# Byte adjacency for layers 1 and 3 of a four-layer graph network, and its float32r copy written in layer 1

## Chip, cores and metric

The kernel runs on one core of one Trainium2 chip. The metric is the device time of one execution in microseconds (us), the median of several. All runs quoted here were in the fast state: none took over 1.5% more than the fastest of the same kernel. A run of the kernel before accompanies every comparison on the same chip, because that kernel's median differs by up to 12 us between groups of runs (4558.7 to 4570.7 us; by 3.5 us between two groups on one chip).

## The reference

Four layers work on X (4096 x 256) and one adjacency matrix of zeros and ones (4096 x 4096), each followed by a residual addition and a normalisation. Cut to what matters here:

```python
def _L1_gnn_ref(x, adj, weight, bias):
    support = x @ weight
    A = DIAG_LAMBDA * jnp.diagonal(adj) + adj
    return A @ support + bias
# layer 2 uses the adjacency too: R = (adj + I) / rowsum, R @ X in two steps
def _L3_gnn_ref(x, adj, W, b):
    deg = jnp.sum(adj, axis=1, keepdims=True)
    agg = adj @ x / jnp.maximum(deg, 1.0)
    return jax.nn.relu(jnp.concatenate([x, agg], axis=-1) @ W + b)
# each layer: x = _layernorm(x + layer(x, ...))
```

Layer 0 is an attention over the edges with eight heads. Layer 2 does two steps of diffusion beside a top-p attention.

## The kernel before

The adjacency arrives as float32, in tiles transposed on the host. Layer 0's first pass (called pz below, after its product) loads it once and makes two things of it in device memory: a float32r copy `adjs` (67 MB), and bytes `nad` (16.8 MB) whose value, read as fp8, is 2^-5 for an edge. Layer 0's main part (acc) reads the bytes. Layers 1, 2 and 3 read `adjs`.

```python
# layer 0, first pass (in a loop over blocks b, pieces g)
a = work.tile([P, 2, G, P], F32, name="a", bufs=2)
for q in range(2):
    nc.sync.dma_start(a[:, q], self.adjt[b + q, :, g * G:(g + 1) * G, :])
ar = work.tile([P, 2, G, P], F32R, name="ar")              # two buffers
nc.vector.tensor_copy(ar, a)
nb = work.tile([P, G, 2, P], U8, name="nb")
for q in range(2):
    nc.scalar.mul(nb[:, :, q, :], a[:, q], float(FIFTH))
    nc.gpsimd.dma_start(self.adjs[b + q, :, g * G:(g + 1) * G, :], ar[:, q].bitcast(F32))
nc.gpsimd.dma_start(nad[it, :, g * G:(g + 1) * G, i:i + 2 * P], nb.rearrange("p g q i -> p g (q i)"))
# ... 32 products from ar into pz
# [cut: layer 0's main part, layer 2]

# adj_product, used by layers 1 and 2
for g in range(self.NB // G):
    a = pool.tile([P, G, P], F32R, name="adj_piece", bufs=bufs)
    nc.sync.dma_start(a.bitcast(F32), self.adjs[...])      # [cut: indices]
    for k in range(G):
        nc.tensor.matmul(ps, a[:, k, :], rhs(g * G + k)..., ...)

# layer 1, after the support product; row = the diagonal's row + bias
for b in range(NB):
    ps = psum.tile([P, 512], F32, name="ps_adj")
    self.adj_product(work, ps, b, lambda jc: XD[:, jc])
    xb = X[:, b:b + 1, :]
    nc.gpsimd.tensor_add(xb[:, 0], xb[:, 0], row)          # "row add"
    nc.vector.tensor_add(xb[:, 0], xb[:, 0], ps[:, :D])
    nc.vector.tensor_add(xb[:, 0], xb[:, 0], ps[:, D:])
    self.layernorm(work, xb, xb)

# layer 3, products of a block, and its closing
for g in range(NB // G):
    a = work.tile([P, G, P], F32R, name="adj_piece", bufs=8)
    nc.sync.dma_start(a.bitcast(F32), self.adjs[b, :, g * G:(g + 1) * G, :])
    for jc in range(g * G, min((g + 1) * G, NB - 1)):
        product(ps, a, jc)
def close(b, ps, a):
    product(ps, a, NB - 1)
    x = work.tile([P, 2, D], F32, name="x", bufs=3)
    nc.scalar.dma_start(x, self.xo[b])
    # [cut: scale on ScalarE, four VectorE operations, layernorm]
    nc.scalar.dma_start(out[:, b, :], y[:, 0])
```

Instructions are put in order by a scheduler, not taken in source order: a row add needs only X and `row`, so the scheduler may put all 32 of them ahead.

## Time and profile before

The kernel takes 4560.47 us (median of three, 4558.66 to 4562.25). The profiled run has a span of 4560.9 us and these stages, read from the first and last start of each product:

| stage | us |
|---|---|
| layer 0, first pass (pz, 4096 products) | 76.4 to 629.2: 552.8 |
| layer 0, main part (acc) | 647.8 to 1377.1: 729.3 |
| layer 1, first support product to last product | 1398.3 to 1691.9: 293.6 |
| layer 2, from there to its last product | 1691.9 to 4281.3: 2589.4 |
| layer 2's last product to layer 3's first | 6.9 |
| layer 3, first to last product | 4288.2 to 4548.9: 260.7 |
| after layer 3's last product | 12.0 |

The prediction below shows the slices, the windows and the waits. One more view is needed for layer 1, the timeline of the kernel before (start, length, engine, source line, operation, tiles, shapes, count, and in brackets the idle time before it and what ended it), first GpSimd's row adds, then the first VectorE instruction after its long idle time:

```profile
1447.23 22.11 POOL L660 TENSOR_TENSOR X<-X,row 128x256 f32<-128x256 f32 x32 [54.98 <-DVE row L654]
...
1469.38 0.29 DVE L769 COPY v<-ident 64x64 f32<-64x64 f32 x2 [15.39 <-POOL X L660]
```

All 32 row adds run in one burst of 22 us, and VectorE stands still for 15 us behind them, in front of a copy that already belongs to layer 2. The early layer 2 load of which the prediction speaks waits for the same burst.

### The profile page before, as it was taken

What the parts mean: (1) busy time and instruction counts of PE and PEld (TensorE: products, weight loads), DVE (VectorE), ACT (ScalarE), POOL (GpSimd) and SP (SyncE); (2) the same over time, 40 slices, a digit from 0 to 9 for tenths busy, and PEclk for the clock granted to TensorE, in tenths of its full rate; (3) what the DMA queues carried; (4) which work ended last, traced back from release to release, by engine and by line L of the source; (5) the groups of instructions that cost most, each with busy time, mean ns of one, the idle gap of its engine ahead of it and who ended that gap; (6) DMA issues with size and microseconds to landing.
All of it is one profiled execution on the core that took longest, in us unless ns stands there. A gap on an engine that the chain in (4) does not pass through costs nothing. (4 is left out here: it accounts for less than half of the span.)

```text
span 4560.9 us, 70953 instructions
## 1 busy us (share of the span) xinstructions
PE 4263.9 (93%) x25625; PEld 3423.7 (75%) x25625; DVE 3254.6 (71%) x7529; ACT 2630.8 (58%) x5373; POOL 458.0 (10%) x794
## 2 busy tenths in 40 slices
PE   8799989999997999999999999887999999999898
PEld 7799989999995876677777777664666666666676
DVE  6532349999993236977777777388989998999133
ACT  5433359998881015766666666267667767775100
POOL 1344420001102100000000000001010000000000
PEclk9999999999998999999999999998999999999899
DMA  5898982342212974012222222530121222222697
GB/s 162 289 312 305 309 303 77 113 147 67 63 62 77 317 261 150 26 62 92 85 80 79 78 81 94 194 111 27 60 73 65 76 74 79 78 79 77 223 318 253
DMA packets 312087, 624.21 MB, mean 137 GB/s; under 512 B 42406, under 2 KB 117926, under 8 KB 311718
## 3 DMA queue, kind: packets, MB, share of 16 engines
q1 hardware_dynamic: 197700, 423.31, 28.3%
q0 software_dynamic: 33344, 107.11, 6.6%
q10 hardware_dynamic: 80674, 89.06, 5.8%
q8 instruction: 207, 3.39, 0.3%
q14 instruction: 162, 1.33, 0.1%
HBM read 464.29 MB, written 155.06 MB: 136 GB/s over the span
## 5 line engine op out<-in xcount | busy, mean ns | idle before, releaser
L1180 PE MATMUL ps_a<-X,aT 128*128 128x256 f32 x4096 | 964.2, 387 | 28.9 <-ACT aT L1177 28.8
L1180 PEld LDWEIGHTS ps_a<-X,aT 128*128 128x128 f32 x4096 | 763.3, 191 | 294.7 <-ACT aT L1177 137.9
L242 PE MATMUL acc<-gm,gt 128*128 128x198 bf16 x8192 | 710.2, 250 | 37.7 <-issue 18.3
L242 PEld LDWEIGHTS <-gt 128*128 128x128 fp8e4 x8192 | 705.2, 98 | 42.7 <-issue 18.5
L234 ACT ACTIVATE sg<-lpb,nlc 128x1024 fp8e4<-128x1024 f32 x640 | 670.5, 1135 | 76.5 <-DVE gt L236 38.3
L450 PE MATMUL pz<-src,ar 128*128 128x264 f32 x4096 | 520.9, 290 | 32.5 <-DVE ar L439 26.0
L450 PEld LDWEIGHTS pz<-src,ar 128*128 128x128 f32 x4096 | 514.7, 192 | 38.6 <-DVE ar L439 31.3
L155 PE MATMUL ps_r<-XD,adj_piece 128*128 128x512 f32 x2048 | 509.9, 401 | 14.1 <-DMA adj_piece<-adjs 13.9
L1177 ACT COPY aT<-ps_tp 128x512 f32<-128x512 f32 x512 | 277.5, 583 | 360.3 <-PE ps_tp L1175 358.1
L915 ACT ACTIVATE ja<-e,nc 128x2048 uint8<-128x2048 f32 x240 | 478.7, 1995 | 0.5 <-issue 0.2
L155 PEld LDWEIGHTS ps_r<-XD,adj_piece 128*128 128x128 f32 x2048 | 382.7, 189 | 114.0 <-DMA adj_piece<-adjs 27.9
L842 PE MATMUL ps_logit<-kT,q 64*128 64x512 f32 x1024 | 462.5, 637 | 4.0 <-ACT e L846 3.9
L861 DVE SCALAR_TENSOR_TENSOR v<-e,c 128x4096 bf16<-128x4096 f32 x100 | 447.2, 4472 | 7.3 <-ACT c L889 6.5
L997 DVE MAX8 cand<-v 128x8 f32<-128x256 f32 x1024 | 360.6, 411 | 2.2
L83 POOL TENSOR_SCALAR ln_var<-ln_mv 128x1 f32<-128x1 f32 (+1 forms) x144 | 53.1, 369 | 3027.3 <-DVE ln_mv L81 2786.3
L1044 DVE SCALAR_TENSOR_TENSOR e<-e,edge 128x512 f32<-128x512 f32 x512 | 347.3, 746 | 1.5
L442 ACT ACTIVATE nb<-a 128x512 uint8<-128x512 f32 x256 | 159.2, 630 | 308.4 <-DMA a<-in_adjt_dram 270.7
L1175 PE MATMUL ps_tp<-ident,e 128*128 128x128 f32 x2048 | 273.3, 275 | 38.9 <-DVE e L1044 26.1
L993 DVE SCALAR_TENSOR_TENSOR v<-e,hi 128x2048 f32<-128x2048 f32 x128 | 300.9, 2351 | 1.7
L1175 PEld LDWEIGHTS ps_tp<-ident,e 128*128 128x128 f32 x2048 | 242.1, 142 | 77.3 <-DVE e L1044 29.5
L846 ACT ACTIVATE e<-ps_logit 128x1024 f32<-128x1024 f32 x256 | 261.2, 1021 | 49.4 <-PE ps_logit L842 34.6
L227 DVE TENSOR_SCALAR sg<-lpb,nlc 128x1024 fp8e4<-128x1024 f32 x384 | 273.6, 749 | 1.7
(300 smaller groups left out, 5079.0 us busy)
## 6 DMA issues: line engine op xcount, KB each, us to landing
adj_piece<-adjs SPq DMA_DIRECT2D x256, 512.0 KB
adj_piece<-adjs SPq DMA_DIRECT2D x512, 256.0 KB
a<-in_adjt_dram SPq DMA_DIRECT2D x256, 256.0 KB
adjs<-ar POOLq DMA_DIRECT2D x256, 256.0 KB, 5.1
na<-nad SPq DMA_DIRECT2D x64, 512.0 KB
nad<-nb POOLq DMA_DIRECT2D x128, 128.0 KB, 4.5
lpb<-lpd POOLq DMA_DIRECT2D x32, 512.0 KB, 4.0
xfd<-part ACTq DMA_DIRECT2D x63, 256.0 KB
```

Of the source, the lines that this page charges most:

```text
L155: nc.tensor.matmul(ps, a[:, k, :], rhs(jc).rearrange("p s d -> p (s d)"), start=(jc == 0 and own is None), stop=(jc == self.NB - 1))
L234: nc.scalar.activation(sg[:, k, :], lpb, AF.Sign, scale=-1.0, bias=nlc[:, jc, h:h + 1], saturate=False)
L242: nc.tensor.matmul(acc[:, q, :6 * C1], gt[:, k, q * P:(q + 1) * P], gm[:, jc, hh, :], start=(jc == 0 and q % 2 == 0), stop=(jc == NB - 1 a ...
L450: nc.tensor.matmul(pz[q][:, t, :W], ar[:, q, k, :], src[:, jc, t, s], start=(jc == 0 and s == 0), stop=(jc == NB - 1 and s == 1))
L842: nc.tensor.matmul(pl[:, s, :], q[s * A:(s + 1) * A, :], kT[s * A:(s + 1) * A, c * 512:(c + 1) * 512], start=True, stop=True)
L861: nc.vector.scalar_tensor_tensor(junk, e, c, e, op0=ALU.is_ge, op1=ALU.mult, accum_out=S)
L915: nc.scalar.activation(ja, e[:, s * HALF:(s + 1) * HALF], f, bias=nc1, accum_out=fs[:, i + s:i + s + 1])
L993: nc.vector.scalar_tensor_tensor(v, ec, hi, ec, op0=ALU.is_lt, op1=ALU.mult, accum_out=sb[:, s:s + 1])
L997: nc.vector.max(cand[:, 8 * j:8 * j + 8], v[:, k * 256:(k + 1) * 256])
L1044: nc.vector.scalar_tensor_tensor(ec, ec, edge[:, j:j + 1], ec, op0=ALU.is_ge, op1=ALU.mult)
L1175: nc.tensor.transpose(pt[:, k * P:(k + 1) * P], e[:, jc * P:(jc + 1) * P], self.ident)
L1180: nc.tensor.matmul(pa[:, :D], aT[:, k * P:(k + 1) * P], X[:, jc, :], start=(jc == 0), stop=(jc == NB - 1))
```

## The change

The intent is to move less data. Layer 0 no longer stores the float copy. Layer 1 loads the bytes (1 MB pieces, on the ScalarE queue), casts them on VectorE and ScalarE in turn, stores each cast piece as part of the float copy for layer 2 (128 stores of 512 KB on the SyncE queue), and multiplies from it. Layer 3 loads bytes and casts them as well; from its third block on, a block's last product also moves from the closing to the place before it. The core of the diff, with the lists that the two helpers fill and return cut:

```diff
 def adj_space(self):
+    self.nad = pool.tile([N // self.IT, P, NB, self.IT], U8, name="nad")
     self.adjs = pool.tile([self.NB, P, self.NB, P], F32, name="adjs")
+def bytes_of(self, pool, b, G=8):
+    for g in range(self.NB // G):
+        na = pool.tile([P, G, self.IT], U8, name="na", bufs=2 * (self.NB // G))
+        self.nc.scalar.dma_start(na, self.nad[b * P // self.IT, :, g * G:(g + 1) * G, :])
+def adj_pieces(self, pool, nas, b, G=8):
+    at = b * P % self.IT
+    if at == 0:
+        nas[:] = self.bytes_of(pool, b)
+    for g in range(self.NB // G):
+        a = pool.tile([P, G, P], F32R, name="adj_piece", bufs=2 * (self.NB // G))
+        edges = nas[g][:, :, at:at + P].bitcast(FP8)
+        if g % 2:
+            nc.scalar.mul(a, edges, 2.0 ** 5)
+        else:
+            nc.vector.tensor_scalar_mul(a, edges, 2.0 ** 5)
 # layer 0
-    nc.gpsimd.dma_start(self.adjs[b + q, :, g * G:(g + 1) * G, :], ar[:, q].bitcast(F32))
 # layer 1
+ahead = self.adj_pieces(work, nas, 0)
 for b in range(NB):
-    self.adj_product(work, ps, b, lambda jc: XD[:, jc])
+    now, ahead = ahead, None
+    for g, a in enumerate(now):
+        nc.sync.dma_start(self.adjs[b, :, g * 8:(g + 1) * 8, :], a.bitcast(F32))
+        ... # eight products from a
+    if b + 1 < NB:
+        ahead = self.adj_pieces(work, nas, b + 1)
 # layer 3
-    nc.sync.dma_start(a.bitcast(F32), self.adjs[b, :, g * G:(g + 1) * G, :])
+pieces = {b: self.adj_pieces(work, nas, b) for b in range(2)}
+    # in the loop: pieces[b + 2] = self.adj_pieces(work, nas, b + 2), ahead of close(b)
```

More of the change, by code (lines that the diff above doesn't have):

```diff
@@ L138, in adj_space @@
     def adj_space(self):
+        N, NB = self.N, self.NB
         pool = self.ctx.enter_context(self.tc.tile_pool(name="adjs", bufs=1, space=DRAM))
+        self.IT = min(1024, N)
+        self.nad = pool.tile([N // self.IT, P, NB, self.IT], U8, name="nad")
         self.adjs = pool.tile([self.NB, P, self.NB, P], F32, name="adjs")
@@ L156, in adj_product @@
                                  start=(jc == 0 and own is None), stop=(jc == self.NB - 1))
+    def bytes_of(self, pool, b, G=8):
+        nas = []
+        for g in range(self.NB // G):
+            na = pool.tile([P, G, self.IT], U8, name="na", bufs=2 * (self.NB // G))
+            self.nc.scalar.dma_start(na, self.nad[b * P // self.IT, :, g * G:(g + 1) * G, :])
+            nas.append(na)
+        return nas
+    def adj_pieces(self, pool, nas, b, G=8):
+        nc = self.nc
+        at = b * P % self.IT
+        if at == 0:
+            nas[:] = self.bytes_of(pool, b)
+        pieces = []
+        for g in range(self.NB // G):
[5 more added lines that the diff above has]
+                nc.vector.tensor_scalar_mul(a, edges, 2.0 ** 5)
+            pieces.append(a)
+        return pieces
     def layer0(self):
@@ L180, in layer0 @@
             lpd = dram.tile([H, N], F32, name="lpd")
-            nad = dram.tile([N // IT, P, NB, IT], U8, name="nad")
+            nad = self.nad
             zd = dram.tile([NB, P, H, C1], F32, name="zd")
@@ L654, in layer1 @@
             nc.vector.tensor_add(row, row, pd[:, D:])
+            nas = []
+            ahead = self.adj_pieces(work, nas, 0)
             for b in range(NB):
                 ps = psum.tile([P, 512], F32, name="ps_adj")
-                self.adj_product(work, ps, b, lambda jc: XD[:, jc])
+                now, ahead = ahead, None
+                for g, a in enumerate(now):
+                    nc.sync.dma_start(self.adjs[b, :, g * 8:(g + 1) * 8, :], a.bitcast(F32))
+                    for k in range(8):
+                        jc = g * 8 + k
+                        nc.tensor.matmul(ps, a[:, k, :], XD[:, jc].rearrange("p s d -> p (s d)"),
+                                         start=(jc == 0), stop=(jc == NB - 1))
+                if b + 1 < NB:
+                    ahead = self.adj_pieces(work, nas, b + 1)
                 xb = X[:, b:b + 1, :]
@@ L1332, in layer3 @@
             out = self.rows(self.out)
+            nas = []
             def product(ps, a, jc):
-                nc.tensor.matmul(ps, a[:, jc % G, :], self.XD[:, jc].rearrange("p s d -> p (s d)"),
+                nc.tensor.matmul(ps, a[jc // G][:, jc % G, :], self.XD[:, jc].rearrange("p s d -> p (s d)"),
                                  start=(jc == 0), stop=(jc == NB - 1))
@@ L1340, in products, with close @@
                 ps = psum.tile([P, 512], F32, name="ps_adj")
-                for g in range(NB // G):
-                    a = work.tile([P, G, P], F32R, name="adj_piece", bufs=8)
-                    nc.sync.dma_start(a.bitcast(F32), self.adjs[b, :, g * G:(g + 1) * G, :])
-                    for jc in range(g * G, min((g + 1) * G, NB - 1)):
-                        product(ps, a, jc)
+                a = pieces.pop(b)
+                for jc in range(NB - 1):
+                    product(ps, a, jc)
                 return b, ps, a
-            def close(b, ps, a):
-                product(ps, a, NB - 1)
+            def close(b, ps, a, done=False):
+                if not done:
+                    product(ps, a, NB - 1)
                 x = work.tile([P, 2, D], F32, name="x", bufs=3)
@@ L1366, in layer3 @@
                 close(*t)
+                pieces[t[0] + 2] = self.adj_pieces(work, nas, t[0] + 2)
             for b in range(2, NB):
-                close(*products(b))
+                t = products(b)
+                product(t[1], t[2], NB - 1)
+                if b + 2 < NB:
+                    pieces[b + 2] = self.adj_pieces(work, nas, b + 2)
+                close(*t, done=True)
 @with_exitstack
```

## The prediction

> **What bounds the kernel now.** I first read the page's slices: matrix work, granted clock, DMA share and bytes moved, 114 us a slice.
>
> ```profile
> PE   8799989999997999999999999887999999999898
> ...
> PEclk9999999999998999999999999998999999999899
> DMA  5898982342212974012222222530121222222697
> GB/s 162 289 312 305 309 303 77 113 147 67 63 62 77 317 261 150 26 62 92 85 80 79 78 81 94 194 111 27 60 73 65 76 74 79 78 79 77 223 318 253
> ```
>
> TensorE (PE) is busy nearly everywhere. DMA comes close to its limit in three places: slices 0 to 5 (layer 0's first pass over the adjacency, to 630 us), 12 to 14 (layer 1, 1397 to 1694) and 37 to 39 (layer 3, 4282 to 4561). The change touches just these. Layer 2, 2.6 ms between them, keeps its work: the compiled order of instructions of the changed kernel differs there only in its first microseconds.
>
> PE's busy share hides small gaps, so the second view is the count of matmuls in equal windows. Layer 0's first pass (columns: window, length, PE busy and count, weight loads, clock, DMA share, GB/s):
>
> ```profile
> 180.00:200.00 20.00, 15.84 (x113) 15.20 (x111) 0.91 0.87 302
> 200.00:220.00 20.00, 15.86 (x123) 15.23 (x124) 1.00 0.84 288
> 300.00:320.00 20.00, 20.00 (x166) 20.00 (x165) 1.00 0.90 303
> 320.00:340.00 20.00, 20.00 (x166) 20.00 (x165) 1.00 0.90 314
> ```
>
> 166 matmuls in 20 us, 120.5 ns each, is what PE does undisturbed. From 80 to 280 us it does only 1277 (the sum of ten such windows), or 157 ns each, with lower clocks in between; from 280 to 630 about 125. The waits of the stretch to 640 us (total us, times, longest) name DMA:
>
> ```profile
> ACT nb L442 <- DMA a<-in_adjt_dram: 270.7, 189, 4.9
> DVE ar L439 <- DMA adjs<-ar: 191.9, 55, 6.9
> PEld pz L450 <- DVE ar L439: 31.3, 24, 3.6
> ```
>
> VectorE's cast waits for the store of its own buffer (two buffers), ScalarE for the loads that share the engines with that store, and PE for the cast.
>
> Layer 1, in windows of 10 us, the same columns:
>
> ```profile
> 1460.00:1470.00 10.00, 3.20 (x15) 2.31 (x13) 0.87 0.00 0
> 1470.00:1480.00 10.00, 5.29 (x17) 4.30 (x18) 0.62 0.82 258
> 1480.00:1490.00 10.00, 9.58 (x40) 6.98 (x39) 1.00 1.00 331
> 1500.00:1510.00 10.00, 10.00 (x46) 8.29 (x45) 1.00 0.90 317
> ```
>
> Steady state is PE at 219 ns a matmul (46 in 10 us), with DMA at 0.9. Before it there is one hole of 12 us with DMA at zero. The order of the SyncE queue explains it: between layer 1's loads stands an early load for layer 2 that waits for GpSimd, which is busy for 22 us adding a row to X.
>
> Layer 3:
>
> ```profile
> 4420.00:4430.00 10.00, 10.00 (x45) 8.11 (x44) 1.00 0.82 266
> 4440.00:4450.00 10.00, 7.74 (x32) 5.93 (x32) 1.00 0.80 257
> 4490.00:4500.00 10.00, 7.28 (x32) 5.61 (x31) 1.00 0.78 256
> ```
>
> 45 in 10 us (222 ns) when it flows, often 32. The closing chain waits for its small load behind the adjacency, which shares the engines (view of waits, 4280 to 4561):
>
> ```profile
> DVE x L1354 <- DMA x<-xo: 139.1, 31, 7.2
> PE ps_adj L1335 <- DMA adj_piece<-adjs: 20.2, 14, 5.8
> ```
>
> **What the Trainium skill says.** "DMA: Bandwidth & Descriptors", Measured, gives a core alone 341 GB/s for 1 MB and 425 for 16 MB; the trace has 288 to 334 in layer 0 and 317 to 365 in layer 1 at shares of 0.84 to 1.01, so some 345 is a fair sustained limit here. "DVE: opcode table, instruction layouts, handler registers and perf-mode slots", Perf-mode slots: an op with one source and an fp8 or fp32 stream reaches the two-port mode, two elements a cycle. The trace agrees: 128x1024 from float32 takes 711 ns into float32r and 749 into fp8, so I take 0.73 us for fp8 into float32r; no run yet shows that pair. "SBUF — State Buffer", SBUF: two separate sides: DMA ports and engine ports do not contend, so 64 MB of stores out of SBUF should not slow PE; layer 0's 120.5 ns beside stores agrees. "TensorE: Matmul & The Clock Gate", What's actually happening: idleness lowers PE's clock; above, 0.62 after the hole. Removed gaps therefore give a little more than their length.
>
> **The change, part by part.**
>
> *Layer 0 loses 256 stores of 256 KB* (67 MB). The pass moved a 512 KB load, 512 KB of copy and 128 KB of bytes for each group of 32 matmuls, plus some 320 KB of other stores per group in its first part: 1.47 MB in 5.0 us. Now it is 0.95 MB; at PE's pace of 3.88 us that asks for 245 GB/s, below the limit. The instruction order on VectorE and ScalarE is unchanged here, so the two-buffer wait vanishes and the loads land sooner. From 80 to 280 us PE did 40 groups: at 3.88 us they take 155 us, 45 less. But VectorE's own work per group is about 3.0 us in a ping-pong with ScalarE (waits of 48 and 22 us for gb), so I take 4.15 us: 34 saved. From 280 to 630, 88 groups at 3.97 can fall to 3.90: 6 saved, part of it not reached. Layer 0: **-38 us**, 20 to 50.
>
> *Layer 1 reads 16.8 MB of bytes and writes 67 MB instead of reading 67 MB.* Casts: 64 on VectorE (0.73 us) and 64 on ScalarE (1.08 us, between 1021 and 1135 ns of other 128x1024 forms): per block of 32 matmuls (7.0 us) VectorE gets 1.5 us on top of 1.9, ScalarE 2.2. Neither bounds. DMA: 84 MB and 4 MB of X. The order shows 8 MB of byte loads and some 6 MB of stores already in the 50 us in which PE makes the support (DMA was at zero there), so 73 MB are left beside about 986 matmuls, 216 us: 339 GB/s against my limit of 345. It is balanced on the edge. The early layer 2 load has left this queue, so the hole of 12 us goes, with about 8 us of slow restart. Against this: casts standing before splits in ScalarE's order while the first bytes land, 3 us, and stores that lag, 5 us. Layer 1: **-14 us**.
>
> *Start of layer 2*: its first adjacency loads were made in layer 1; now they wait until all stores have landed and the pools are released: **+4 us**.
>
> *Layer 3 reads 16.8 MB instead of 67.* DMA falls to about 29 MB in 250 us, so the small loads return in time. The start is later: 1 MB of bytes at 345 GB/s (3 us), 2 us latency and a cast, so PE starts near 4290.5 instead of 4288.1, and the fourth piece of the first block arrives about 4299, so that block ends near 4302. Then 992 matmuls at 222 ns take 220 us: 4522, and the last closing chain 10 us: 4532 against 4561. In ScalarE's order a cast now stands behind the output of the block before, and that loop (scale, three VectorE adds with casts between, normalisation, output, cast) is about 6.9 us by its durations, too close to PE's 7.1: I take 4 us off. Layer 3: **-25 us**.
>
> Sum: -38 -14 +4 -25 = -73 us, so 4560 - 73 = **4487 us**, 1.6% less.
>
> **Rivals.**
> *Stores bound layer 1.* If stores with loads sustain only 300 GB/s, 73 MB take 243 us instead of 216; casts wait for buffers, PE idles and its clock dips. Layer 1 then ends some 10 us later than before, and the whole is about 4511. For it: the mixed layer 0 stood at 303 to 314. Against: there PE set the pace.
> *Layer 0 is held by the chain, not by stores.* If the ping-pong of VectorE and ScalarE is the bound to 280 us, only 15 us come back: 4510. For it: gb waits of 70 us. Against: most begin behind a ScalarE instruction that waits for a load.
> *All becomes PE-bound.* Layer 0 gives 50, layer 1 with no lag 22, layer 3 29: about -100, 4460, just over 2%.
>
> **Range and chances.** The three parts scatter by about 11, 11 and 6 us, together 17 or so; with some allowance for the unknown the range is 4458 to 4516. Over 2% faster needs below 4471, one deviation away: 0.25. Slower by 2% would need 90 us of new waits, and no part offers them: 0.02. Within 2%: 0.73.
>
> **What would show it.** Layer 0's matmuls from 80 to 280 us should rise from 1277 to about 1540, with no wait of VectorE on a store. In layer 1 the DMA share should be near 1 with about 340 GB/s, the hole gone, 44 to 46 matmuls per 10 us; many waits of casts on stores would prove the first rival. Casts should measure 0.73 and 1.08 us: at 1.2 us on VectorE nothing moves in layer 1, but layer 3's loop would become the bound. Layer 3 should show few 32s, DMA below 0.5, and its last matmul 25 us earlier relative to its first. Layer 2 should keep its length within 5 us. The prediction is wrong if layer 2 changes, or stores run far below loads.

## The result

The changed kernel takes 4505.26 us (median of four, 4500.63 to 4508.22) against 4561.36 us for the kernel before on the same chip. The ratio is 0.9876, with a 95% interval from 0.9859 to 0.9893. Ratios here are the mean time of one kernel's fast runs over that of the other's of the same rounds, so not quite the ratio of the medians. The change is worth 1.2%, or 56 us.

| stage (profiled runs) | before | after | difference |
|---|---|---|---|
| layer 0's first pass and all before layer 1's first support product | 1398.3 | 1364.8 | -33.5 (pass alone -32.9) |
| layer 1 | 293.6 | 290.1 | -3.5 |
| layer 2 | 2589.4 | 2586.3 | -3.1 |
| layer 2's last product to layer 3's first | 6.9 | 10.5 | +3.6 |
| layer 3, first to last product | 260.7 | 239.9 | -20.8 |
| after it | 12.0 | 7.3 | -4.7 |
| span | 4560.9 | 4498.9 | -62.0 |

The page's slices of the changed kernel (112 us a slice), to be set against the ones that the prediction shows:

```profile
PE   8999989999987999999999999887999999999799
...
DMA  4655553332215964022222222530122222222541
GB/s 132 226 198 178 176 201 106 97 139 64 88 37 206 385 235 139 27 78 85 81 79 80 79 81 84 200 118 30 39 78 77 80 79 80 68 70 76 189 143 48
```

DMA in layer 0's pass has fallen from some 300 GB/s to 176 to 226. In slice 13 (layer 1) it has risen to 385. Layer 3 (the last three slices) needs 189, 143 and 48.

Layer 0's pass in windows (window, length, PE busy and count, weight loads, clock, DMA share, GB/s):

```profile
180.00:200.00 20.00, 18.02 (x133) 17.62 (x132) 0.91 0.69 219
200.00:220.00 20.00, 19.09 (x153) 18.56 (x152) 1.00 0.71 229
...
300.00:320.00 20.00, 20.00 (x166) 20.00 (x165) 1.00 0.54 181
```

From 80 to 280 us the ten windows sum to 1522 products (before: 1277). From 240 us on the pass is full. The waits to 640 us confirm that VectorE no longer waits for a store, but for PE, which is now the slower one:

```profile
ACT nb L472 <- DMA a<-in_adjt_dram: 280.2, 151, 4.0
DVE ar L469 <- PE pz L479: 231.5, 79, 3.2
```

Totals over 640 us hide where the time was lost. Nearly all of the gain lies between 80 and 280 us (245 more products, some 30 us at 120.5 ns each). There VectorE's cast had waited for the store of its own buffer for only 6.8 of its 191.9 us; the rest came after 280 us, where PE waited 1.5 us for the cast. Another wait was long in the stretch of the gain: ScalarE waited for the store of `gb`, a piece of the factored rows, and VectorE, whose casts stand in order behind, waited for ScalarE. The waits from 80 to 280 us, before:

```profile
DVE ar L439 <- DMA adjs<-ar: 6.8, 3, 3.7
ACT gb L420 <- DMA gmd<-gb: 28.0, 18, 4.3
DVE vf L421 <- ACT gb L420: 48.0, 27, 4.2
```

And after:

```profile
ACT gb L450 <- DMA gmd<-gb: 7.2, 10, 1.7
DVE vf L451 <- ACT gb L450: 28.4, 23, 4.2
```

PE's own wait for the cast falls with them, from 24.5 to 7.9 us. This is read from waits; no run moved the store of `gb` alone.

Layer 1 in windows of 10 us (PE, weight loads, VectorE, ScalarE, GpSimd, each busy us and count; clock, DMA share, GB/s):

```profile
1420.00:1430.00 10.00, 10.00 (x45) 8.26 (x45) 3.35 (x7) 1.06 (x1) 8.83 (x13) 1.00 0.39 157
1430.00:1440.00 10.00, 2.69 (x12) 1.88 (x10) 9.25 (x1) 0.00 (x0) 10.00 (x16) 0.83 0.00 0
1440.00:1450.00 10.00, 7.27 (x24) 5.83 (x25) 7.47 (x14) 3.06 (x3) 6.82 (x11) 0.66 0.51 196
1450.00:1460.00 10.00, 10.00 (x46) 8.29 (x45) 4.86 (x12) 3.66 (x4) 0.78 (x2) 1.00 1.02 398
...
1550.00:1560.00 10.00, 10.00 (x46) 8.29 (x45) 3.91 (x9) 3.18 (x3) 0.78 (x2) 1.00 1.03 417
```

The hole is still there, about as long as before: 36 products in the 20 us from 1430 us, where 90 would fit. In its first half VectorE is busy for 9.25 us with **one** instruction. Afterwards PE runs at its steady 46, with loads and stores at 398 to 417 GB/s. The timeline of the same stretch names that instruction:

```profile
1430.75 11.05 DVE L91 TENSOR_SCALAR X<-X,ln_mv,ln_rstd 128x256 f32<-128x256 f32 x1 [6.21 <-POOL ln_rstd L84]
...
1430.69 10.97 POOL L700 TENSOR_TENSOR X<-X,row 128x256 f32<-128x256 f32 x16
...
1442.16 0.42 DVE L702 TENSOR_TENSOR X<-X,ps_adj 128x256 f32<-128x256 f32 x1
```

And in the waits of layer 1 (total us, times, longest), the line of PE's hole:

```profile
PE ps_adj L695 <- DVE X L702: 10.0, 1, 10.0
```

A normalisation of 128x256, which takes 0.41 us elsewhere, started 0.06 us after GpSimd began sixteen row adds, and ended when they ended. It had already waited 6.21 us for a small GpSimd step behind twelve earlier row adds. Behind it in VectorE's order stand block 1's two additions of the product (L701, L702), which free one of layer 1's two PSUM buffers for block 3. PE had finished three blocks (96 products) and waited for that buffer: its 10.0 us end with L702. It did not wait for casts, as the author believed when the next runs were planned: the first three pieces of block 3 had been cast by 1424.54 us. The Trainium skill's "SBUF — State Buffer", SBUF: two separate sides, describes something that fits: VectorE in a two-port mode and GpSimd share a pair of ports as "an **exclusive lock**", held "for the whole instruction". The trace agrees in kind. It does not agree in extent: this VectorE instruction waited for sixteen GpSimd instructions, not for one, while in the eleven row adds just before (from 1421.17 us) a cast got in after one at most, with 0.88 us in place of 0.68. VectorE's additions with PSUM kept their 0.42 us in the burst.

Layer 3 is now steady, with DMA far from its limit (columns as for layer 1; before, the window from 4440 us had 32):

```profile
4430.00:4440.00 10.00, 10.00 (x44) 8.10 (x43) 5.36 (x12) 2.53 (x4) 0.92 (x3) 1.00 0.22 70
4440.00:4450.00 10.00, 10.00 (x44) 8.10 (x43) 4.97 (x12) 3.90 (x5) 0.77 (x2) 1.00 0.13 42
```

The casts are as cheap as thought, by the view of each line (VectorE: least, median and longest ns) and by the page's group (ScalarE: busy us and mean ns):

```profile
L184 DVE TENSOR_SCALAR adj_piece<-na x128: 675/693/1218, 1367.8 to 4475.3; 128x1024 fp32r<-128x1024 fp8e4 x128
```

```profile
L182 ACT ACTIVATE adj_piece<-na 128x1024 fp32r<-128x1024 fp8e4 x128 | 135.2, 1059 | 326.5 <-PE ps_adj L695 128.4
```

### The profile page after: what moved, and what is told of

The parts are those of the page before. It is cut to its first block, busy times and chain, and to the rows that moved or that the text cites. A ratio compares the mean times of both kernels' runs of the same rounds, so it can differ in the third digit from the quotient of the medians.

```text
span 4498.9 us, 70573 instructions
## 1 busy us (share of the span) xinstructions
PE 4245.9 (94%) x25625; PEld 3417.3 (76%) x25625; DVE 3342.9 (74%) x7657; ACT 2758.4 (61%) x5501; POOL 313.6 (7%) x538
## 5 line engine op out<-in xcount | busy, mean ns | idle before, releaser
L479 PE MATMUL pz<-src,ar 128*128 128x264 f32 x4096 | 510.7, 287 | 9.8 <-DVE ar L469 7.9
L182 ACT ACTIVATE adj_piece<-na 128x1024 fp32r<-128x1024 fp8e4 x128 | 135.2, 1059 | 326.5 <-PE ps_adj L695 128.4
```

The source lines that it names most:

```text
L479: nc.tensor.matmul(pz[q][:, t, :W], ar[:, q, k, :], src[:, jc, t, s], start=(jc == 0 and s == 0), stop=(jc == NB - 1 and s == 1))
```

## The experiments

Twelve kernels ran, all correct. Each group shared one chip and its runs of the kernel before. "Layer 1" and "layer 3" are first to last product as in the table above.

| run | time, us | before there, us | ratio (95%) | pz pass | layer 1 | gap to layer 3 | layer 3 | tail |
|---|---|---|---|---|---|---|---|---|
| kernel before | 4561.4 | | 1 | 552.8 | 293.6 | 6.9 | 260.7 | 12.0 |
| changed kernel | 4505.3 | 4561.4 | 0.9876 (0.9859 to 0.9893) | 519.9 | 290.1 | 10.5 | 239.9 | 7.3 |
| row_vector | 4492.4 | 4570.7 | 0.9825 (0.9807 to 0.9843) | 521.5 | 278.6 | 10.4 | 239.9 | 7.3 |
| row_late | 4495.5 | 4570.7 | 0.9828 (0.9810 to 0.9845) | 523.4 | 279.6 | 10.5 | 240.2 | 8.0 |
| before_row_vector | 4554.0 | 4570.7 | 0.9954 (0.9937 to 0.9970) | 563.9 | 280.1 | 7.5 | 265.4 | 11.0 |
| layer3_only | 4549.3 | 4570.7 | 0.9951 (0.9934 to 0.9967) | 564.9 | 292.6 | 10.9 | 239.9 | 7.3 |
| stores_in_layer0 | 4545.2 | 4558.7 | 0.9967 (0.9955 to 0.9979) | 558.0 | 290.5 | 10.3 | 239.8 | 7.4 |
| layers01_only | 4503.7 | 4558.7 | 0.9879 (0.9864 to 0.9894) | 521.2 | 288.2 | 7.1 | 243.3 | 8.3 |
| layer0_buffers | 4503.1 | 4558.7 | 0.9874 (0.9859 to 0.9888) | 522.7 | 290.8 | 10.4 | 240.8 | 7.3 |
| layer3_start | 4505.7 | 4558.7 | 0.9883 (0.9868 to 0.9898) | 521.1 | 290.4 | 10.7 | 244.3 | 7.9 |
| before_placed | 4564.8 | 4565.3 | 1.0000 (0.9989 to 1.0010) | 562.0 | 292.8 | 7.3 | 259.4 | 10.0 |
| layers01_placed | 4507.6 | 4565.3 | 0.9875 (0.9859 to 0.9892) | 524.6 | 291.1 | 7.0 | 241.2 | 7.3 |
| best | 4494.4 | 4565.3 | 0.9846 (0.9833 to 0.9860) | 520.8 | 277.2 | 9.0 | 245.1 | 7.3 |
| written_twice | 4561.9 | 4561.7 | 1.0000 (0.9988 to 1.0011) | 555.7 | 290.3 | 7.2 | 265.6 | 9.2 |

### What makes the hole in layer 1

Three kernels move the row adds. The first is the changed kernel with this edit:

```diff
-                nc.gpsimd.tensor_add(xb[:, 0], xb[:, 0], row)
+                nc.vector.tensor_add(xb[:, 0], xb[:, 0], row)
```

> The changed kernel, with the 32 row adds of layer 1 on VectorE instead of GpSimd; nothing else. Theory 1 (the burst of GpSimd's row adds holds VectorE's two-port instructions, the normalisation at 11.05 us instead of 0.41, and through VectorE's order the casts): the hole in layer 1 (36 matmuls in the 20 us from 1430 us, where 90 would fit) goes, no VectorE instruction in layer 1 lasts over 2 us, and layer 1 from its first transpose to its last product becomes 8 to 13 us shorter than 292.0 us; the whole is 8 to 13 us below the changed kernel's 4505 us, about 4494. Theory 2 (the hole is the start of the stream of bytes, casts and stores, and the row adds only happen to stand there): the hole stays within 3 us and the time stays at 4502 to 4507 us.

The second leaves the row add on GpSimd, after the additions of the product, where it depends on each block and so cannot run ahead:

```diff
-                nc.gpsimd.tensor_add(xb[:, 0], xb[:, 0], row)
                 nc.vector.tensor_add(xb[:, 0], xb[:, 0], ps[:, :D])
                 nc.vector.tensor_add(xb[:, 0], xb[:, 0], ps[:, D:])
+                nc.gpsimd.tensor_add(xb[:, 0], xb[:, 0], row)
```

> The changed kernel, with each row add left on GpSimd but placed after the two additions of the product, so that the 32 adds can no longer run in one burst ahead of the blocks; the sums are the same up to rounding. Theory 1 (it is the burst, not the engine, that makes the hole): hole gone as with the adds on VectorE, layer 1 8 to 12 us shorter than 292.0 us, single waits of VectorE on GpSimd up to 1.5 us, whole about 4495 us. Theory 2 (the start of the stream): hole and time stay within 3 us.

The third makes the first edit in the kernel before:

> The kernel before, with the 32 row adds of layer 1 on VectorE instead of GpSimd; nothing else. Theory 1 (the same burst made the hole before the change too, there through the early layer 2 load and a VectorE copy that both wait for GpSimd): the hole (45 matmuls in the 23 us from 1457 us) goes and layer 1, 295.4 us from its first transpose to its last product, becomes 9 to 14 us shorter; the whole is about 4550 us, 0.2 to 0.3 per cent below the kernel before. Theory 2 (the hole before was only the place of the early load in the SyncE queue, waiting for something besides the row adds): less than 3 us.

Theory 1 held in all three, except for the casts in it (PE waited for the additions, as shown above): layer 1 lost 11.5, 10.5 and 13.5 us. The third kernel as a whole fell by 0.46%, more than the 0.2 to 0.3 expected. The hole is gone; windows with the row adds on VectorE, columns as for layer 1 above:

```profile
1430.00:1440.00 10.00, 10.00 (x45) 8.29 (x45) 8.47 (x25) 2.12 (x2) 1.74 (x4) 1.00 0.75 295
1440.00:1450.00 10.00, 10.00 (x45) 8.26 (x45) 7.44 (x20) 4.06 (x4) 0.78 (x2) 1.00 0.73 281
```

The normalisation, in layer 1 and the last few microseconds of layer 0 of the run with late row adds (times from the view of its line: least, median and longest ns), no longer has a long case, although GpSimd does as many row adds:

```profile
L91 DVE TENSOR_SCALAR X<-X,ln_mv,ln_rstd x36: 405/413/416, 1360.0 to 1654.6; 128x256 f32<-128x256 f32 x36
```

So it is the burst, not the engine. The burst made the hole before the change too; it only reached PE by another road first, the early load of layer 2 in the SyncE queue: PE stopped after 80 products, and its 11.51 us ended with a load. The road through VectorE was there as well: block 1's additions, behind the copy of layer 2, ended at 1471.52 us, so with the load alone out of the way PE could have run 16 more products and would then have waited for a PSUM buffer.

### Whether the parts add, and where the stores cost time

The kernel before with only layer 3 changed:

> The kernel before, with only layer 3 changed: it reads the bytes and casts them; layer 0 still writes the float copy, and layers 1 and 2 read it. By the stage comparison of the two traces (layer 3's matmuls from 260.7 to 239.9 us, tail from 12.0 to 7.3 us, start 3.7 us later) the gain is 22 us, so about 4539 us with layers 0 to 2 unchanged. If the gain of layer 3 needed the rest of the change (fewer stores earlier), it would be under 12 us.

It gained 21.5 us of medians, as expected, with layer 3 at 239.9 us. Next, the stores put back into layer 0 (`nc.gpsimd.dma_start(self.adjs...)` as before, and the store in layer 1 deleted):

> The changed kernel, but the float copy is written in layer 0 as before (256 stores of 256 KB), and layer 1 reads and casts the bytes without storing anything. It separates the two places of the stores. Theory A (the stores cost time only in layer 0, where loads of the same size run beside them; in layer 1 they are hidden): the first pass of layer 0 goes from about 520 us back to 553 to 565 us, and layer 1, 290.1 us from first support product to last product, stays within 3 us; the whole is 33 to 45 us above the changed kernel, about 4540 to 4550 us. Theory B (the rival of the prediction, stores bound layer 1 as well): layer 1 becomes 6 us or more shorter without them, so the whole rises by less than 30 us.

Theory A held: the pass went back to 558.0 us and layer 1 stayed at 290.5 us. In layer 1, 67 MB of stores cost nothing that shows; the prediction's first rival is out. Then the changed kernel with layer 3 as it was before:

> The changed kernel with layer 3 as it was before (reads the float copy). If the parts add, layer 3 takes 261 to 265 us with a tail of 11 to 12 us and starts 7 us after layer 2, so the whole is about 22 us above the changed kernel: 4527 us. If layer 3's gain and the rest interact (the last stores in another place, another order of buffers), the difference is under 12 us or over 32 us.

This missed. Its time of 4503.7 us is that of the whole change. Layer 3, with exactly the code of the kernel before, took 243.3 us and not 261 to 265. The change in layer 3 is worth 21.5 us alone, and nothing that shows once the other parts are there: the parts do not add.

### Why old layer 3 code is faster once layer 0 stores less

Three kernels ask what the difference is. First, the kernel before with the bytes placed ahead of the float copy in device memory, as the change has it, and no instruction changed:

```diff
+        self.nad = pool.tile([N // self.IT, P, NB, self.IT], U8, name="nad")
         self.adjs = pool.tile([self.NB, P, self.NB, P], F32, name="adjs")
-            nad = dram.tile([N // IT, P, NB, IT], U8, name="nad")
+            nad = self.nad
```

> The kernel before, with one thing of the change: the bytes are allocated in device memory ahead of the float copy of the adjacency, in the same pool, which moves the float copy by 16.8 MB; no instruction changes. The question: layer 3 with its old code took 243.3 us in the run with layers 0 and 1 alone changed, but 260.7 and 265.4 us in the kernel before and in the one with row adds on VectorE. Theory P (place of the float copy in device memory): layer 3 takes 241 to 247 us here, and the whole is 12 to 20 us below the kernel before. Theory W (who wrote the copy: stores of 4 KB per partition in layer 1 instead of 2 KB in layer 0, or the traffic before) or theory C (differences between chips and runs): layer 3 stays at 258 to 267 us and the whole within 5 us.

Second, layers 0 and 1 changed and layer 3 old, with the bytes allocated after everything that lay there before:

```diff
-        self.nad = pool.tile([N // self.IT, P, NB, self.IT], U8, name="nad")   # before adjs
+        pool = self.ctx.enter_context(self.tc.tile_pool(name="nads", bufs=1, space=DRAM))
+        self.nad = pool.tile([self.N // self.IT, P, self.NB, self.IT], U8, name="nad")   # after xo
```

> Layers 0 and 1 changed and layer 3 as before, as in the run of that name, but the bytes allocated after the float copy and X's output, so that both lie where they lay before the change. Theory P (place in device memory): layer 3 goes from 243.3 back to 258 to 267 us and the whole to about 4520 us. Theory W (who wrote the copy): layer 3 stays at 241 to 247 us and the whole at 4500 to 4506 us. Theory C (chips and runs): layer 3 is the same as in the run with the kernel before and moved bytes, which goes to the same chip, within 4 us, whichever it is.

Layer 3 took 259.4 and 241.2 us on one chip. So the place in device memory is not it, nor the chip. Third, layers01_only with one line more, layer 0's old store, so that the copy is written twice with the same values:

```diff
+                        nc.gpsimd.dma_start(self.adjs[b + q, :, g * G:(g + 1) * G, :], ar[:, q].bitcast(F32))
```

> The float copy is written twice, with the same values: in layer 0 as before the change and again in layer 1 as after it; layer 3 is as before and reads the float copy. Place in device memory and chips are ruled out for layer 3's two durations (259 to 265 us after layer 0 wrote the copy, 241 and 243 us after layer 1 wrote it); this asks whether the last writer decides, or what layer 0's 256 stores leave behind. Theory L (the last writer: a copy written in pieces of 4 KB per partition through the SyncE queue reads faster): layer 3 takes 241 to 247 us, 4 KB reads there last 178 to 183 ns in the mean, and the whole is near 4545 us. Theory H (what the 256 stores of the GpSimd queue leave behind, whoever writes last): layer 3 takes 257 to 267 us, the reads 186 to 190 ns, and the whole is near 4560 us. In both, layer 0's first pass takes 553 to 565 us.

Theory H held: layer 3 went to 265.6 us, though layer 1 wrote last, and though in the two traces TensorE, VectorE, ScalarE, GpSimd and SyncE carry out the same instructions in the same order in layer 3 as in layers01_only. All of layer 3 as one window (window, length, then busy us and count of PE, weight loads, VectorE, ScalarE and GpSimd; clock, DMA share, GB/s), for layers01_placed:

```profile
4257.70:4498.90 241.20, 241.19 (x1024) 193.89 (x1024) 83.46 (x218) 14.68 (x31) 24.17 (x62) 0.99 0.91 326
```

And for written_twice:

```profile
4286.90:4552.50 265.60, 247.12 (x1024) 193.22 (x1024) 82.49 (x216) 14.59 (x31) 23.36 (x60) 0.99 0.86 297
```

The same reads come at 326 and at 297 GB/s. At PE's steady 222 ns a block of 32 products takes 7.1 us and moves 2.5 MB (2.1 MB of adjacency, 0.26 MB of X and its product, 0.13 MB of output), some 350 GB/s. Old layer 3 therefore stands on an edge, and a small loss of rate turns into idle PE: busy for 241.19 of 241.20 us above, 18.5 us idle here. The trace's packet records show the loss: reads of 4096 bytes in layer 3 last 187.0 to 188.5 ns in the mean in the four profiles with stores in layer 0 and the old layer 3 (kernel before, before_row_vector, before_placed, written_twice), and 179.2 and 182.2 ns in the two without (layers01_placed, layers01_only). The median is 159 ns in all six; only the tail differs. Layer 2's reads of the same copy, of 2048 bytes, do not divide the runs so: 99.7 ns in written_twice, 99.6 and 98.8 in the two without. How the 256 stores of the GpSimd queue act more than three milliseconds later these runs do not tell; they may leave something behind, or act through the 30 us by which they delay all that follows. Their count, their queue and their bytes were not varied apart from one another, so this stays **open**. It is shown that they cause it, not how.

### What still holds layer 0's pass, and the start of layer 3

A third buffer for the adjacency load of the pass (`name="a", bufs=3`; the prologue's x gives up one):

> The changed kernel with three buffers instead of two for the adjacency load of layer 0's first pass (x of the prologue loses its third buffer to make room). It asks what still holds the pass from 100 to 260 us, where 1197 of about 1328 possible products run. Theory A (the latency of the loads: ScalarE waits 70.6 us for them from 76 to 280 us): the third buffer lifts the count and the pass shrinks by 6 to 14 us from 520 us. Theory B (the chain of VectorE and ScalarE for the factored rows, which is in program order and knows no buffer of this load): the pass changes by less than 3 us.

The pass took 522.7 us, within 3 us of the others, which is Theory B's number. A deeper load buffer is not what the missing 138 products of 80 to 280 us wait for (1522 of about 1660). That the chain of VectorE and ScalarE holds them fits its waits for each other, but was not tried by itself.

The byte loads of layer 3's first blocks on the SyncE queue, in halves of 512 columns:

```diff
+            for i in range(0, self.IT, 512):
+                for g in range(self.NB // G):
+                    self.nc.sync.dma_start(nas[g][:, :, i:i + 512],
+                                           self.nad[b * P // self.IT, :, g * G:(g + 1) * G, i:i + 512])
```

> The changed kernel with the first byte loads of layer 3 issued on the SyncE queue in halves of 512 columns, the halves that block 0 needs first. Theory A (the late and slow start of layer 3 is the issue behind ScalarE's last output and the full 4 MB ahead of the first block's last piece): layer 3 starts 2 to 4 us earlier after layer 2 than the changed kernel's 10.5 us, and its 239.9 us become 2 to 5 us shorter; the whole is 4 to 8 us below 4505 us. Theory B (the load's buffers are released only when layer 2's last output has been read, whichever queue issues): the start stays at 9.5 to 10.5 us and only the halves help, 2 to 4 us in all.

Both theories missed in part. The start stayed at 10.7 us (B), but the halves did not help: layer 3 took 4.4 us more. In the DMA view they moved at 290 GB/s for about 7 us, where the whole pieces of the changed kernel move at 403 to 440.

A version meant to win combines the row adds on VectorE with two first blocks of layer 3 read from the float copy:

```diff
-                nc.gpsimd.tensor_add(xb[:, 0], xb[:, 0], row)
+                nc.vector.tensor_add(xb[:, 0], xb[:, 0], row)
-            pieces = {b: self.adj_pieces(work, nas, b) for b in range(2)}
+            pieces = {b: whole(b) for b in range(2)}          # loads from self.adjs on SyncE
+            nas[:] = self.bytes_of(work, 0, queue=nc.sync)
```

> A version meant to beat both: the changed kernel with the row adds on VectorE, and in layer 3 blocks 0 and 1 read from the float copy through the SyncE queue, which needs no cast and no full 4 MB ahead of the first block; the bytes of the other blocks come behind them in the same queue. If the late start of layer 3 is the 4 MB and the cast, layer 3 starts about 7 us after layer 2 instead of 10.5, its first two blocks run without gaps, and 239.9 us become 228 to 234: 9 to 15 us in all below the version with row adds alone, about 4480 us. If the start is bound by something else, 4487 to 4493 us as with the row adds alone.

It took 4494.4 us, a miss: better than both kernels of the case, but not than row_vector, from which its ratio can't be told, and with layer 3 at 245.1 us. Layer 3 started 9.0 us after layer 2, ran 80 products, and then stood for 3 us, since the bytes had been put behind the float pieces. The version to keep is row_vector, one word away from the changed kernel: 4492.4 us, 1.75% below the kernel before.

## Why the prediction was right or wrong

It gave 4487 us, 4458 to 4516, and 0.73 for "within 2%". The measured 4505 us lie in the range, 18 us above the middle. By its own terms:

- **Layer 0, -38.** Measured -33.5. The cause is right: the stores were the cost (stores_in_layer0 brings it back), and the count of 80 to 280 us rose to 1522 against "about 1540". The wait that it named is not: "VectorE's cast waits for the store of its own buffer" is 6.8 us in the stretch that gained. What fell there are ScalarE's wait for the store of `gb` (28.0 to 7.2 us, and 23.1 with the stores put back) and VectorE's waits for ScalarE behind it. So the "ping-pong" that the prediction took as fixed was itself lengthened by the stores. The size varies between profiles: with the stores the pass takes 553 to 565 us (562.0 and 555.7 on one chip), without them 520 to 525.
- **Layer 1, -14.** Measured -3.5. The step that failed is "The early layer 2 load has left this queue, so the hole of 12 us goes". The load was one of two roads from GpSimd's burst to PE; the other runs through VectorE's additions, which free the PSUM buffers. The profile before already showed it, VectorE idle for 15.39 us behind the same burst. The prediction named GpSimd's 22 us and then removed only the queue order. With the burst gone as well, layer 1 is 293.6 - 278.6 = 15.0 us shorter than before, close to the predicted -14. (The terms that the prediction lists, 12 + 8 - 3 - 5, give 12.)
- **The limit of 345 GB/s**, and with it "balanced on the edge" and the first rival, was too low. Layer 1 moved 365 to 417 GB/s in each of the six windows from 1450 us, and taking its stores away changed nothing. The profile before already had a window of 413 GB/s, from 4290 to 4300 us. The prediction's "317 to 365 in layer 1" also leaves out windows of 291 to 315 in which PE ran undisturbed: there the rate was what the kernel asked for, not a limit.
- **Start of layer 2, +4.** Not there: layer 2, from layer 1's last product, is 3.1 us shorter, which is within the scatter of all fourteen profiles (2584.3 to 2589.7).
- **Layer 3, -25.** Measured +3.6 - 20.8 - 4.7 = -21.9. Steady 44 to 45 per window, DMA at 0.12 to 0.65 from 4280 to 4480 us, and casts of 0.69 and 1.06 us, all about as said; PE started a little later than worked out (10.5 us after layer 2 against 9.2, with a latency of 2 us that rests on no trace). But the reasoning missed that old layer 3 was slowed by layer 0's stores. The gain would have come without reading bytes there: 243.3 us with the old code. Nor was "the closing chain waits for its small load" the cost: in layers01_placed that wait is still 114.4 us (139.1 before) and PE runs through; what fell is PE's own wait for the adjacency, from 20.2 to 6.0 us. The size was right by luck in part: without layer 3 the prediction's parts sum to -48, and layers01_only gained 55.0 us of medians.
- **Second rival** (layer 0 held by the chain): what is missing there, 138 products or about 17 us of PE's time, may be its part; it was not tried by itself. **Third rival** (all PE-bound): not reached, because of the hole, the late start of layer 3 and that remainder.

## What to carry to other kernels

A wait that one removes is often one of several roads from the same cause: before crediting its length, look at what else stands still behind the same instruction. Work that a scheduler may run ahead on GpSimd (here 32 additions that depend on nothing late) can hold VectorE, and everything in order behind it, so tie such work to its block or put it elsewhere. When a change has several parts, run each part alone in both directions: here two parts were each worth the same 20 us, and it was there to be had only once. And read a wait in the stretch where the time is lost, not in a total over the stage: the longest wait of layer 0's cast stood where PE hardly waited for it.

## What the Trainium skill lacked or had wrong

- "SBUF — State Buffer", SBUF: two separate sides: the shared ports are said to be held for the whole instruction. A VectorE normalisation of 0.41 us took 11.05 us beside sixteen GpSimd additions in a row, so a row of them can hold it throughout; in another burst of eleven, a VectorE cast came in after one at most (0.88 us instead of 0.68). The page doesn't say which of the two to expect, and these runs don't either.
- "DMA: Bandwidth & Descriptors", Measured: the table, for loads issued from GpSimd, has no rate for loads and stores in flight together. Here 1 MB loads and 512 KB stores from the ScalarE and SyncE queues moved 365 to 417 GB/s in six windows of 10 us in a row. The table itself isn't contradicted: its 425 GB/s for 16 MB is the nearer of the two figures, and taking the 341 for 1 MB as a sustained limit made the prediction's first rival look likelier than it was.
- No page read for this study has it: after 256 stores of 256 KB through GpSimd's queue in layer 0, reads of 4 KB through the SyncE queue more than three milliseconds later last 187.0 to 188.5 ns in the mean instead of 179.2 and 182.2, and a layer that needs nearly the whole rate takes 259 to 266 us instead of 241 to 243. The cause is open.
